# Moving single waits: the order of work in a four-layer graph kernel on one Trainium2 core

## The chip, the cores and the metric

The kernel runs on one core of a Trainium2 chip. A core has a matrix engine (TensorE, PE in the profile; PEld is its weight load), a vector engine (VectorE, DVE), an engine for activations (ScalarE, ACT), a general engine (GpSimd, POOL) and queues that issue DMA transfers; here SyncE (SP) and ScalarE issue them. Each engine runs its own list of instructions in order and waits at semaphores for the others. The metric is the device time of one execution in microseconds (us), the median of several.

## The reference

3327 nodes with 256 features pass four pre-norm residual layers. A is the 3327 x 3327 adjacency matrix `adj`, about 1% of it nonzero.

```python
h = relu(layernorm(x)); x = x + adj @ (h @ W0.T + b0)                              # layer 0
h = relu(layernorm(x)); x = x + relu(top700(tanh(adj*adj)) @ (tanh(h @ Wp + bp) @ Wg) + bg)   # layer 1
h = relu(layernorm(x)); x = x + relu(D**-.5 (adj + I) D**-.5 @ (h @ W2.T))          # layer 2
h = relu(layernorm(x)); x = x + gnn(h)                                              # layer 3

# gnn: two steps
R = (adj + I) / rowsum
for n in range(2):
    logits = (Xa @ W1.T @ W2.T) @ (Xa @ W3.T).T
    A  = softmax(logits) kept to the largest entries that hold 0.9 of the row, renormalised
    Xf = R @ Xf;  Xa = A @ Xa
    Z += Xf @ U1[n].T + Xa @ U2[n].T
gnn = layernorm(h + Z) * g + b
```

D is the row sum of adj + I. All arithmetic that the kernel does on these is float32.

## The kernel before

**Tiles.** The nodes are padded to 26 blocks of 128. Blocks p and p + 13 form *pair* p, so there are 13 pairs. In layers 0 to 2 a pair's rows of `adj` meet the node features as a 2 x 2 block product done with seven block products instead of eight (Strassen in Winograd's form). For that, sums of the four blocks of `adj` are made on VectorE (`Feed.adding`, L552 to L555: s1, a21, s2, s4) and sums of the node blocks once per layer (`combining_nodes`, L367 to L370). The 13 blocks along the inner dimension are cut in three (`CUTS`: 0-5, 5-9, 9-13). So a product of one pair has 91 *units* (7 times 13 matmuls of 128 x 128 x 128), counted 0 to 90; `Product.steps` issues them (L601) in the order 1, 2, 5, 4, 7, 3, 6, in which 5 needs s1, 3 needs s4 and 6 needs s2.

**Loading.** `Feed.upto(n)` keeps the loads two cuts and the sums one cut ahead of the product: it issues the loads of `adj` (L528, four per cut, on SP's queue), then for each load a count of the positive entries where the layer counts (`counter`, L715 to L722, VectorE), then the sums, and stores those sums that layer 3 uses again (L577). `done` (L727, L728) adds a pair's counts with one matmul and copies them out.

**Results.** `Product.result` copies one accumulator bank by ScalarE (L617) and makes the four blocks on VectorE (L622 to L627). Then `finish` adds bias and residual, and the next layer's `Pair` measures and norms its rows (L387, L388, root on POOL L114 and L116, L404; in layer 3 also L459). Its *stages* - turning by TensorE (L416, evicted by L420), projection, and in layer 3 the keys and queries (`keys`, L269, L277, L281) - are hung into the units of the next pair's product by number: `WHERE`, `WHERE_FIRST` for the first pair of a layer, `WHERE_KEYS` in layer 2. In layers 1 and 2 the first cut of pair 1's product is done early, within pair 0's (`early`), since the last node block arrives last.

**Start.** `first_two` runs the first two pairs' products together, in a written order, after `busy` matmuls of the identity (L797) and the 13 pairs' norm, turn and projection.

**Layer 3.** The keys are centred by their mean (`key_sum` L1011 and L1015, `centre` L1022 and L1025). Per row block m of the first step: logits in four chunks (L1045), exponentials by ScalarE (L1070), a search for the threshold (`search_steps`: two passes over the row on ScalarE, L1103 and L1108, or the second on VectorE for row 0, then VectorE L1119 to L1148), then `Rows.begin` transposes the first two groups (L202, copied by ScalarE, L205) and `Rows.finish` does seven groups of matmuls (L213), transposing ahead. In between, `propagate_first` does R @ Xf by pairs in two phases (L1277); `half` (L1286) copies the first bank, and `whole` (L1296 to L1303) makes the blocks. `propagate_first(n, at)` takes a plan: a number k of 26 says behind which share of the phase's units a step is issued. Rows listed in `APART` have no phase behind them and follow each other directly. The second step does the same in the order of pairs, with `finish_pair` or `finish3` making the final layer norm and storing the output (L1397).

**Who sets the order.** TensorE's order is the program's (`tc.manual_schedule(engines=PE_ALONE)`), and so are VectorE's, ScalarE's and SP's inside `first_two`. Elsewhere a planner orders the other engines' instructions before the run, by program order and its own estimate of times; `tc.high_priority()` lifts instructions, and `tc.issue_after(x)` puts those of a block behind x on x's engine.

Of the kernel before, what the change touches and what calls it, by code (L numbers as in the profile page):

```python
# [11 lines left out]
F32 = mybir.dt.float32  # L12
# [5 lines left out]
ALU = mybir.AluOpType  # L18
# [29 lines left out]
def kernel(  # L48
# [243 lines left out]
    def layers_0_to_2(again):  # L292
# [115 lines left out]

        evicted = []

# [23 lines left out]
        class Pair:  # L434
# [17 lines left out]
            def apply(self):  # L452
                if self.layer == 3:
                    self.xn = pair_of(self.rhs.rows, self.p)
                else:
                    self.xn = work.tile([P, 2, D], F32, tag="xn", name=f"xn_{self.name}")
                normed(self.name, self.x2, self.xn, self.mv, self.r, split=self.layer == 0)
                if self.layer == 3:
                    self.made = nc.vector.tensor_scalar(self.xn, self.xn, 0.0, None, ALU.max)  # L459
# [49 lines left out]
        class Feed:  # L509
# [33 lines left out]
            def adding(self, p, c):  # L543
# [12 lines left out]
                if (p, c) in self.keep:  # L556
                    at = self.order.index((p, c))
                    self.made += [(at, s_dram[:, p, n, a:b, :], s) for n, s in enumerate((s1, s2, a21, s4))]
                self.ready[p, c] = a11, a12, s4, a22, s1, s2, a21
                yield last  # L560

# [21 lines left out]
        class Product:  # L583
# [24 lines left out]

            def result(self):

# [5 lines left out]
                with tc.high_priority():  # L616
# [4 lines left out]
                    p1, p2, p5 = (p3[:, n, :P] for n in range(3))  # L621
                    nc.vector.tensor_tensor(u[:, 2, :], p1, b[:, 0, :], ALU.add)  # L622
                    nc.vector.tensor_tensor(u[:, 1, :], u[:, 2, :], b[:, 1, :], ALU.add)
# [8 lines left out]
        WHERE = {2: (60, 84), 3: (48, 61, 76), 6: (12, 22, 34, 46, 58, 70)}  # L632
        WHERE_KEYS = (74, 89)
        WHERE_FIRST = {2: (58, 86), 3: (52, 70, 89)}

        def products(layer, width, rhs, feed, finish, before, pair_after, following=None, counted=None, begin=None):
# [5 lines left out]
            for p in range(H):  # L642
# [4 lines left out]
                else:  # L647
# [36 lines left out]
                    feed.upto(n)  # L684
                y, p3 = prod.result()
                x2 = feed.x2.pop(p)
# [18 lines left out]
        def counter(i):  # L705
# [18 lines left out]
            def done(p):  # L724
                m = p + i * H
                pc = bank(f"pc_{m}")
                nc.tensor.matmul(pc[:, :1], sums.pop(p)[:, 0, :], ones, start=True, stop=True)  # L727
                nc.vector.tensor_copy(counts[:, m : m + 1], pc[:, :1])  # L728

# [30 lines left out]
        if not again:  # L760
# [33 lines left out]
            def first_two(product):  # L794
                busy = bank("busy")
                for _ in range(12):
                    nc.tensor.matmul(busy[:, :P], ident, ident, start=True, stop=True)  # L797
                with tc.manual_schedule(engines=IN_FIRST_TWO):
                    return first_two_in(product)

            def first_two_in(product):
                for a, b in ((0, 1), (1, 2), (2, 4), (4, 6), (6, 9), (9, 12), (12, 13)):
# [38 lines left out]
                for p in range(H):  # L841
                    pairs[p].turn()
                    if p + 3 < H:
                        pairs[p + 3].measure()
# [31 lines left out]
                count()  # L876
                feed.to_count = None
                feed.upto(5)
                work_of(4)
                work_of(5)  # L880
                return len(order), prods

# [97 lines left out]
    def layer_3_in(again, tag, big, ep, w3, sm3, h3, kT0, ksum0, left):  # L980
# [244 lines left out]
        class PropagatedPair:  # L1225
# [79 lines left out]

            def ended(self):
                with tc.high_priority():
                    nc.vector.tensor_tensor(self.y[:, 1, :], self.y[:, 1, :], self.accs[2][:, :P], ALU.add)

# [90 lines left out]

        ys, stores = {}, []

        def finish_pair(p, both, pair):
# [162 lines left out]
        with tc.manual_schedule(engines=PE_ALONE):  # L1566
# [88 lines left out]
            for i in range(EARLY):  # L1655
# [11 lines left out]
                elif i == 1:  # L1667
                    steps = prepare(0, 0, kT0)
                    centred = {4: [lambda: centre(kT0, mean0(), "0"), lambda: next(sums_of_first)]}
                    propagate_first(1, merged(centred, whole_run(steps, 10), plan))  # L1670
                    run(find(0, 0, st0))
# [11 lines left out]
            for m in range(T):  # L1683
# [7 lines left out]
                if m + AHEAD < T and not interleaved:  # L1691
                    plan = merged(plan, {4: [lambda: next(prepare(0, m + AHEAD, kT0))]})
                a = AttentionOfFirstStep(m, rows.finish(m, plan), dens.pop(m), f"{m}")
                if interleaved:
# [57 lines left out]
        with tc.manual_schedule(engines=PE_ALONE):  # L1752
# [31 lines left out]
            for i, m in enumerate(ORDER):  # L1784
                ahead = ORDER[i + AHEAD] if i + AHEAD < T else None
                plan, later = passes_apart(1, finder) if ahead else (passes(finder), {})
                if i == 0:
                    p, q = props
                    plan = merged(plan, {5: [p.scale, q.scale]})
                    of_next = {2: [p.turn], 5: [q.turn], 10: [p.sums], 14: [q.sums]}  # L1790
# [29 lines left out]
                else:  # L1820
# [104 lines left out]
```

## Time and profile before

| | |
|---|---|
| time, median of 3 | 2533.23 us (2530.99 to 2536.49) |
| profiled execution: its time / its span | 2532.95 us / 2531.1 us |
| TensorE busy | 2493.5 us |
| VectorE busy | 2093.9 us |
| ScalarE busy | 1085.2 us |
| POOL busy | 297.7 us |
| layers 0 to 2 | until about 949 us |
| first step of layer 3 | until about 1804 us |
| second step, and the end | until 2531 us |
| last matmul ends | 2519.75 us |
| mean granted TensorE clock | 0.996 |

In a profile line a time stands first as the start in us from the span's beginning, then the duration, engine, line of the kernel, operation, tiles written and read, shapes. `[1.04 <-ACT eT_a L205]` behind it is how long the engine sat idle just before and what released it. A matmul of float32 is recorded as two passes, so one unit is "x2". PEclk is the TensorE clock granted, 1.00 is full.

### The profile page before, as it was taken

How to read it: one execution, taken by the hardware profiler on the slowest of the kernel's cores; microseconds unless marked ns; L12 is line 12 of the kernel's file. 1: busy time of each engine (PE TensorE's matmuls, PEld its weight loads, DVE VectorE, ACT ScalarE, POOL GpSimd, SP SyncE). 2: the span in 40 equal slices, each digit the busy share in tenths (PEclk: the TensorE clock that was granted, in tenths of full speed). 3: DMA queues.
4: the chain of work that ended last, by engine and by line, in shares of the span. 5: the costliest groups of instructions: out<-in, count | busy, mean ns of one | idle time of the engine just before them, and what ended most of it. 6: DMA issues, size and time to landing. Idle time of an engine off the chain costs nothing.

```text
span 2531.1 us, 47787 instructions
## 1 busy us (share of the span) xinstructions
PE 2493.5 (99%) x17953; PEld 2257.0 (89%) x17953; DVE 2093.9 (83%) x5534; ACT 1085.2 (43%) x2158; POOL 297.7 (12%) x463
## 2 busy tenths in 40 slices
PE   9999999999999999999999999999999999999998
PEld 8999999999999998888887888888888888888887
DVE  7777788888877878788879797884999999999995
ACT  3011023444111105565656565663655555565551
POOL 2000010000000001000000000000022222222222
PEclk9999999999999999999999999999999999999999
DMA  6677665555698867323132323133434343344333
GB/s 195 212 225 244 220 207 171 180 173 178 228 314 276 272 224 228 98 82 107 57 112 87 109 84 104 55 107 107 164 104 129 108 132 125 108 127 139 123 114 107
DMA packets 181774, 388.28 MB, mean 153 GB/s; under 512 B 19741, under 2 KB 78746, under 8 KB 181530
## 3 DMA queue, kind: packets, MB, share of 16 engines
q1 hardware_dynamic: 153210, 364.31, 44.5%
q10 hardware_dynamic: 28320, 20.80, 2.6%
q8 instruction: 143, 2.34, 0.4%
q14 instruction: 101, 0.83, 0.1%
HBM read 315.44 MB, written 67.89 MB: 151 GB/s over the span
## 4 chain that ended last, share of the span: by engine, by line
PE 59%; ACT 2%; DVE 1%; issue 0%; POOL 0%; POOLq 0%; DVEq 0%; ACTq 0%
PE a L213 23%; PE f1a L1277 10%; PE f0a L1277 9%; PE pl_a L1045 6%; PE pt_a L202 6%; PE u L1361 2%; PE u L1331 2%; PE f L1204 1%; ACT junk_a L1108 1%; PE pkq L269 0%; ACT junk_a L1103 0%; PE pt_a L162 0%; PE pt_f L162 0%; ACT eT_a L205 0%; ACT e_a L1070 0%
## 5 line engine op out<-in xcount | busy, mean ns | idle before, releaser
L205 ACT COPY eT_a<-pt_a 128x512 f32<-128x512 f32 (+1 forms) x364 | 196.6, 555 | 374.5 <-PE pt_a L202 373.3
L213 PE MATMUL a<-h3a,eT_a 128*128 128x256 f32 x1352 | 324.1, 381 | 1.7 <-ACT eT_a L205 1.7
L213 PE MATMUL a<-vs,eT_a 128*128 128x256 f32 x1352 | 320.3, 381 | 1.3 <-ACT eT_a L205 1.3
L1132 DVE MAX8 cand_a<-w 128x8 f32<-128x128 f32 x1352 | 287.9, 278 | 4.3
L213 PEld LDWEIGHTS a<-h3a,eT_a 128*128 128x128 f32 x1352 | 243.9, 189 | 35.7 <-ACT eT_a L205 3.4
L601 PE MATMUL acc_a<-tsa,s_a 128*128 128x128 f32 (+1 forms) x2028 | 272.5, 276 | 2.7 <-DVE s_a L552 2.7
L213 PEld LDWEIGHTS a<-vs,eT_a 128*128 128x128 f32 x1352 | 244.8, 190 | 31.6 <-ACT eT_a L205 2.0
L601 PEld LDWEIGHTS acc_a<-tsa,s_a 128*128 128x128 f32 x2028 | 250.8, 193 | 3.5 <-DVE s_a L552 2.9
L601 PE MATMUL acc_a<-tsa,a_a 128*128 128x128 f32 x2028 | 249.6, 275 | 0.0
L601 PE MATMUL acc_a<-rhs,a_a 128*128 128x128 f32 (+1 forms) x2028 | 248.5, 276 | 0.7 <-ACT rhs L490 0.7
L601 PEld LDWEIGHTS acc_a<-tsa,a_a 128*128 128x128 f32 x2028 | 239.0, 192 | 0.6
L601 PEld LDWEIGHTS acc_a<-rhs,a_a 128*128 128x128 f32 x2028 | 236.4, 192 | 1.6 <-ACT rhs L490 1.1
L1128 DVE SCALAR_TENSOR_TENSOR w<-e_a,t_a 128x896 f32<-128x896 f32 x208 | 225.5, 1084 | 3.0
L1246 POOL TENSOR_TENSOR slab3a<-slab3a,ident 128x128 f32<-128x128 f32 x100 | 109.8, 1098 | 911.2 <-DMA slab3a<-in_adj_t_dram 340.3
L1070 ACT ACTIVATE e_a<-pl_a 128x1024 f32<-128x1024 f32 x260 | 184.7, 728 | 43.8 <-PE pl_a L1045 38.3
L202 PE MATMUL pt_a<-ident,e_a 128*128 128x128 f32 x1352 | 198.6, 272 | 0.2
L1119 DVE SCALAR_TENSOR_TENSOR w<-e_a,t_a 128x3328 uint8<-128x3328 f32 x52 | 191.6, 3685 | 4.7 <-DVE t_a L1116 0.5
L1148 DVE SCALAR_TENSOR_TENSOR e_a<-e_a,all_least 128x3328 f32<-128x3328 f32 x52 | 192.1, 3694 | 1.8
L202 PEld LDWEIGHTS pt_a<-ident,e_a 128*128 128x128 f32 x1352 | 165.4, 141 | 29.4 <-ACT eT_a L205 2.6
L745 ACT ACTIVATE a_a<-a_a 128x640 f32<-128x640 f32 (+1 forms) x156 | 101.4, 666 | 170.1 <-DVE a_a L743 149.4
L420 ACT ACTIVATE xT_a<-pt_a 128x512 f32<-128x512 f32 x52 | 30.8, 593 | 334.0 <-PE pt_a L416 271.6
L1277 PE MATMUL f0a<-tsa,slab3a 128*128 128x128 f32 x1352 | 165.9, 276 | 0.0
(256 smaller groups left out, 4226.0 us busy)
## 6 DMA issues: line engine op xcount, KB each, us to landing
slab3a<-s_dram SPq DMA_DIRECT2D x100, 832.0 KB, 4.5
a_a<-in_adj_t_dram SPq DMA_DIRECT2D x312, 256.0 KB, 4.3
slab3a<-in_adj_t_dram SPq DMA_DIRECT2D x79, 832.0 KB, 4.6
a_a<-in_adj_t_dram SPq DMA_DIRECT2D x156, 320.0 KB, 3.9
s_dram<-s_a SPq DMA_DIRECT2D x78, 256.0 KB, 4.8
s_dram<-s_a SPq DMA_DIRECT2D x39, 320.0 KB, 4.7
x_dram<-x_a ACTq DMA_DIRECT2D x39, 256.0 KB, 3.2
s_dram<-a_a SPq DMA_DIRECT2D x26, 256.0 KB, 5.2
```

The lines of the kernel that those rows point to most:

```text
L202: nc.tensor.transpose(pt[:, j, :], e[:, k * P : (k + 1) * P], ident)
L205: last_turned.append(nc.scalar.copy(eT[:, : len(blocks), :], pt[:, : len(blocks), :]))
L213: nc.tensor.matmul(acc[:, :width], ready[g][:, j, :], rhs[:, k, :], start=(k == 0), stop=(k == T - 1))
L601: nc.tensor.matmul(self.acc[:, g, at : at + wide], quads[n][:, k - CUTS[c][0], :], t, start=(k == 0 and n in (1, 4)), stop=(k == H - 1 and ...
L1045: nc.tensor.matmul(parts[h], q[h * DA : (h + 1) * DA, :], kT[h * DA : (h + 1) * DA, a:b], start=True, stop=True,)
L1070: last_exp.append(nc.scalar.activation(dst, src, AF.Exp, accum_out=parts[:, c : c + 1]))
L1119: nc.vector.scalar_tensor_tensor(junk, e, t, e, ALU.is_lt, ALU.mult, accum_out=got)
L1128: nc.vector.scalar_tensor_tensor(w[:, : (b - a) * P], eg, t, eg, ALU.is_lt, ALU.mult, accum_out=below[:, g : g + 1])
L1132: nc.vector.max(cand[:, 8 * k : 8 * k + 8], w[:, (k - a) * P : (k - a + 1) * P])
L1148: nc.vector.scalar_tensor_tensor(e, e, least, e, ALU.is_ge, ALU.mult, accum_out=st["kept"][:, m : m + 1])
L1246: added.append(nc.gpsimd.tensor_tensor(x[:, p, :], x[:, p, :], ident, ALU.add))
L1277: nc.tensor.matmul(self.accs[bank][:, c * P : (c + 1) * P], a, self.right(n, k), start=start, stop=last.get(bank) == (n, k), skip_group_ch ...
```

## The change

1. Twelve identity matmuls at the start become 15, and four more are issued behind the first pair's turn.
2. In the first two pairs' written order, the third pair's sums are put ahead of the counts of its loads, which now come behind both products' last cuts; the first result's first sum (L622) is issued behind those sums.
3. The copy of a count (L728) gets high priority.
4. The last pair's `hidden` and `second` stages in layer 1's first product move from units 70 and 89 to 66 and 83.
5. In layers 1 and 2, at the end of the first pair, the feed goes one cut further before the result, and that pair's norm (L404) is issued behind the sums so added.
6. In layer 2 the turn and the keys move from units 74 and 89 to 81 and 90.
7. In layer 3's second phase, the keys' mean moves from 4 to 7.5 of 26 and row 0's logits from 10 to 14.5.
8. For rows of the first step that follow each other, `rows.begin(m + 1)` moves into the row before, behind its sixth group of matmuls.
9. Between the steps, the second row's logits move from 0 to 8 of 26, and the scale, turn and sums there from 3, 8, 12 to 9, 16, 20.
10. In the second step's first row, the first pass of the search for the third row moves from behind group 0 to behind group 4.
11. At the end, the last pair's two rows: the first is stored at once, and the last row is done by `finish_last`, which takes the row's second half with the last bank added straight into z, so that `ended` (L1308) falls away, and makes the statistics by halves.

```diff
-        evicted = []
+        evicted, hold = [], []
...
-                normed(self.name, self.x2, self.xn, self.mv, self.r, split=self.layer == 0)
+                with tc.issue_after(hold[-1].ins) if hold else nullcontext():
+                    normed(self.name, self.x2, self.xn, self.mv, self.r, split=self.layer == 0)
...
+                self.added = last
                 yield last
...
-            def result(self):
+            def result(self, behind=None):
...
-                    nc.vector.tensor_tensor(u[:, 2, :], p1, b[:, 0, :], ALU.add)
+                    with tc.issue_after(behind.ins) if behind else nullcontext():
+                        nc.vector.tensor_tensor(u[:, 2, :], p1, b[:, 0, :], ALU.add)
...
-        WHERE_KEYS = (74, 89)
-        WHERE_FIRST = {2: (58, 86), 3: (52, 70, 89)}
+        WHERE_KEYS = (81, 90)
+        WHERE_FIRST = {2: (58, 86), 3: (52, 66, 83)}
...
-                y, p3 = prod.result()
+                hold[:] = []
+                if early and p == 0:
+                    feed.upto(n + 1)
+                    hold.append(feed.added)
+                y, p3 = prod.result(feed.added if begin and p == 0 else None)
...
-                nc.vector.tensor_copy(counts[:, m : m + 1], pc[:, :1])
+                with tc.high_priority():
+                    nc.vector.tensor_copy(counts[:, m : m + 1], pc[:, :1])
...
-                for _ in range(12):
-                    nc.tensor.matmul(busy[:, :P], ident, ident, start=True, stop=True)
+                def warm_up(n):
+                    for _ in range(n):
+                        nc.tensor.matmul(busy[:, :P], ident, ident, start=True, stop=True)
+                warm_up(15)
...
                     pairs[p].turn()
+                    if not p:
+                        warm_up(4)
...
                 count()
-                feed.to_count = None
                 feed.upto(5)
                 work_of(4)
                 work_of(5)
+                while feed.to_count:
+                    count()
+                feed.to_count = None
...
-            def ended(self):
-                with tc.high_priority():
-                    nc.vector.tensor_tensor(self.y[:, 1, :], self.y[:, 1, :], self.accs[2][:, :P], ALU.add)
...
+        def finish_last(m, y, rows, acc, name, behind):
+            z = w3.tile([P, D], F32, tag="z", name=f"z1_{name}")
+            x3 = w3.tile([P, NC, P], F32, tag="hT", name=f"x3_{name}").rearrange("p c n -> p (c n)")
+            with tc.issue_after(behind.ins):
+                nc.sync.dma_start(z, z_dram[:, m, :])
+                nc.sync.dma_start(x3, x3_dram[:, m, :])
+            nc.gpsimd.tensor_tensor(z, z, y, ALU.add)
+            nc.gpsimd.tensor_tensor(x3, x3, bs, ALU.add)
...
+            with tc.high_priority():
+                nc.vector.scalar_tensor_tensor(z, rows, by, z, ALU.mult, ALU.add)
+                nc.vector.bn_stats(st[:, 0, :], z[:, :P])
+                nc.vector.scalar_tensor_tensor(z[:, P:], acc, by, z[:, P:], ALU.mult, ALU.add)
+                nc.vector.bn_stats(st[:, 1, :], z[:, P:])
+                nc.vector.bn_aggr(mv3, st)
+                nc.vector.tensor_scalar(r, mv3[:, 1:2], EPS, None, ALU.add)
+            rsqrt(r, r)
+            nc.vector.scalar_tensor_tensor(z, z, mv3[:, 0:1], gs, ALU.subtract, ALU.mult)
+            nc.vector.scalar_tensor_tensor(z, z, r, x3, ALU.mult, ALU.add)
+            nc.sync.dma_start(out[m * P : (m + 1) * P, :], z)
...
-                    centred = {4: [lambda: centre(kT0, mean0(), "0"), lambda: next(sums_of_first)]}
-                    propagate_first(1, merged(centred, whole_run(steps, 10), plan))
+                    centred = {7.5: [lambda: centre(kT0, mean0(), "0"), lambda: next(sums_of_first)]}
+                    propagate_first(1, merged(centred, whole_run(steps, 14.5), plan))
...
+                alone = not interleaved and m != T - 3 and m + 1 < T
+                if alone:
+                    plan = merged(plan, {5: [lambda: rows.begin(m + 1)]})
...
-                elif m + 1 < T:
-                    rows.begin(m + 1)
+                elif alone:
                     left_over = {0: [a.turn], 1: [a.node], 3: [a.values]}
...
-            propagate_first(T - 2, merged(whole_run(steps_of_second, 0), {3: [lambda: p.scale(last_exp)], 8: [p.turn], 12: [p.sums]}))
+            propagate_first(T - 2, merged(whole_run(steps_of_second, 8), {9: [lambda: p.scale(last_exp)], 16: [p.turn], 20: [p.sums]}))
...
-                    plan = merged(plan, {5: [p.scale, q.scale]})
+                    plan = merged({4: plan[0]}, {5: [p.scale, q.scale]})
...
-                            stores.append(finish3(m, ys.pop(m), both[:, 1, :], f"{m}", pair.loaded))
-                            pair.ended()
-                            stores.append(finish3(p, ys.pop(p), both[:, 0, :], f"{p}", pair.loaded))
+                            finish3(m, ys.pop(m), both[:, 1, :], f"{m}", pair.loaded)()
+                            finish_last(p, ys.pop(p), both[:, 0, :], pair.accs[2][:, :P], f"{p}", pair.loaded)
```

More of the change, by code (lines that the diff above doesn't have):

```diff
@@ L795, in first_two, with first_two_in @@
                 busy = bank("busy")
-                for _ in range(12):
-                    nc.tensor.matmul(busy[:, :P], ident, ident, start=True, stop=True)
+                def warm_up(n):
+                    for _ in range(n):
+                        nc.tensor.matmul(busy[:, :P], ident, ident, start=True, stop=True)
+                warm_up(15)
                 with tc.manual_schedule(engines=IN_FIRST_TWO):
-                    return first_two_in(product)
-            def first_two_in(product):
+                    return first_two_in(product, warm_up)
+            def first_two_in(product, warm_up):
                 for a, b in ((0, 1), (1, 2), (2, 4), (4, 6), (6, 9), (9, 12), (12, 13)):
@@ L1401, in layer_3_in @@
         ys, stores = {}, []
+        def finish_last(m, y, rows, acc, name, behind):
[6 more added lines that the diff above has]
+            nc.gpsimd.tensor_tensor(x3, x3, bs, ALU.add)
+            st = sm3.tile([P, 2, 6], F32, tag="st3", name=f"st3_{name}")
+            mv3 = sm3.tile([P, 2], F32, tag="mv3", name=f"mv3_{name}")
+            r = sm3.tile([P, 1], F32, tag="r3", name=f"r3_{name}")
+            by = rinv[:, m : m + 1]
+            with tc.high_priority():
[9 more added lines that the diff above has]
+            nc.sync.dma_start(out[m * P : (m + 1) * P, :], z)
         def finish_pair(p, both, pair):
```

## The prediction

> **What bounds the kernel.** I read the page's busy table first, then TensorE's waits, then its timeline around each wait, then the granted clock by window. The page:
>
> ```profile
> span 2531.1 us, 47787 instructions
> PE 2493.5 (99%) x17953; PEld 2257.0 (89%) x17953; DVE 2093.9 (83%) x5534; ACT 1085.2 (43%) x2158; POOL 297.7 (12%) x463
> ```
>
> TensorE is idle for 2531.1 - 2493.5 = 37.6 us in all. Its last matmul ends at 2519.75, so 11.4 us of that are the tail; the rest are single waits, which the view of waits lists (engine, line, who released it; total us, times, longest us):
>
> ```profile
> PE pt_a L416 <- DVE xn_a L404: 3.5, 3, 1.9
> PE pt_a L416 <- DVE h3a L459: 3.1, 2, 1.6
> PE pl_a L1045 <- ACT e_a L1070: 3.0, 1, 3.0
> PE a L213 <- ACT eT_a L205: 3.0, 9, 1.0
> PE acc_a L601 <- DVE s_a L555: 3.0, 3, 2.4
> PE acc_a L601 <- DVE s_a L552: 2.7, 1, 2.7
> PE pk_mean_0a L1011 <- DVE ktotal_0a L1015: 1.5, 1, 1.5
> ```
>
> No wait repeats row by row, except 0.24 to 0.29 us in eight attention rows. So the change can be costed wait by wait. Each wait may cost twice, since the clock can fall behind it. The windows view (stretch; length, PE busy, instructions, granted clock, DMA share, GB/s), cut at the clock's own steps:
>
> ```profile
> 8.10:11.52 3.42, 1.67 (x8) 1.00 1.06 358
> 11.52:14.93 3.41, 3.41 (x11) 0.50 1.11 326
> 697.60:701.01 3.41, 1.05 (x10) 1.00 1.01 358
> 701.01:704.42 3.41, 3.41 (x17) 0.50 0.96 329
> 786.34:789.75 3.41, 1.78 (x17) 1.00 0.06 22
> 789.75:793.16 3.41, 3.41 (x31) 1.00 0.88 245
> ```
>
> A stretch busy for 1.67 us or less is followed by 3.41 us at half clock, which loses 1.7 us; one busy for 1.78 is not. The same follows the waits at 83.83 and 1772.06. Four such stretches cost 6.8 us.
>
> **A rule against this.** The Trainium skill, page "TensorE: Matmul & The Clock Gate", section "Why this matters for your kernels", asks only for no idle gaps above about 3 us, and its Part 1 lets the clock fall after a whole idle window of 3.4 us. By that, none of our gaps but 3.01 us comes near, the warm-up matmuls buy nothing, and the sum below would be 13.5 instead of 18.6 us (2519.5 us). The rows show the fall at half an idle window; I take the rows. That page also says the window runs free of the kernel, so the cost differs by run: a gap of g us between 1.7 and 3.4 fills half a window in g/3.41 of the alignments, my estimate from the 3.41 us above.
>
> **The change, part by part** (gain in us; a unit is one 128-wide matmul, 0.223 us from "x10 1.28" rows).
>
> 1. *Warm-ups.* 3 + 4 identity matmuls are 14 passes of 0.11 = 1.6 us, inside the idle 5.97-7.12 and 7.86-9.81, which stay: both end with xn (L404), which waits for x landing at 6.0 and 8.7. If x came sooner, they would cost up to 1.6. The second gap shrinks to about 1.0 us, so the half clock at 11.52 goes: -1.7 (0 to -1.9). It carries on: VectorE has 0.6 to 1.0 us free per pair until 21.7, then needs 2.18 per pair against TensorE's 2.17.
>
> 2. *Third pair's sums.* The wait at 83.83 (2.66 us) is for L552, which ran at 85.63 behind two counts; the first count reuses the buffer that the count matmul at 81.30 frees. The inputs had landed by 71.0. Put ahead, the sums run from 72.5; L554 waits for the product that ends at 75.05, so L555 ends at 76.5-77. The first result (u, L622, 75.77 before) is queued behind it: 1.3 us later, and behind u the finish, the statistics, the normed pair and its x1 store. Its accumulator is needed at 81.36 only; its turn comes at unit 12, about 84.2, and xn (81.77 before) is ready by 83.1-84.2 with u of the second pair and the counts in between. I keep 0.3 of a wait: -(2.66 + 1.7 - 0.3) = -4.0 (-2.3 to -4.4).
>
> 3. *Layer 1's start.* The count's copy now goes first, but the 0.70 us at 352.77 has a second releaser: the weights come from h2T, whose tanh ends at 353.23 for a load at 353.43. -0.1. The 0.73 us at 382.72 waits for the last pair's projection; issued 6 units (1.3 us) sooner, its copy (L490, 382.81) ends before it is wanted, if tanh L483 (379.25) moves with it: -0.6 (0 to -0.73).
>
> 4. *Sums ahead of the normed pair in layers 1 and 2.* In layer 1, s4 then fills VectorE's 0.91 us wait for the root: -0.5. In layer 2, s4 (L555, 700.15) is wanted at 698.52; wait 2.36 plus 1.7 of clock. Four loads and two counts of the next cut come ahead too. The sums' inputs landed by 690.2 and their buffers are free once stores land at 691.0-693.4, so s4 is there by 695. But these 2.6 us of VectorE go ahead of the finish: the count matmul's wait at 693.45 grows from 0.32 to about 1.0, and h3a (698.1 before) is late by some 1 us at its turn, which must no longer wait at 698.52 but comes at 699.4. -(4.06 - 1.7) = -2.4 (-0.4 to -4.1).
>
> 5. *Keys' turn at 81 for 74.* 7 units are 1.56 us; the two waits are 1.63 and 1.43: -2.9. The keys' matmuls at 90 leave 9 units, 2.0 us, for a copy that ends 1.3 us after the turn starts; the two hT stores and two qT stores on ScalarE's queue move along, in a layer where ScalarE is mostly idle.
>
> 6. *Keys' sum at 7.5, logits at 14.5.* The 1.46 us at 961.79 vanish, since 7 units take 1.56. But the logits still wait for the centred keys (L1025 ends at 967.38), so the exponentials and row 0's first pass stay where they are:
>
> ```profile
> 974.29 3.07 ACT L1103 ACTIVATE junk_a<-e_a,t_a 128x3328 uint8<-128x3328 f32 x1
> 977.27 0.19 ACT L1103 ACTIVATION_READ_ACCUMULATOR junk_a<-e_a,t_a 128x1 f32 x1
> 977.65 0.59 ACT L1286 COPY xf_0a<-f0a 128x512 f32<-128x512 f32 x1 [0.20 <-PE f0a L1277]
> ```
>
> The phase now has 22 units behind the logits for 31: it ends at 970.42 + 4.9 + 0.3 = 975.6 for 977.61. The copy L1286 that frees its bank is then caught behind the pass until 977.46, so TensorE waits from 975.6 to 978.1 (0.68 us before, now 2.5): net -0.2, and that wait brings the half clock, +1.7. I take +1.5 (-1.5 to +1.7). Were the copy put first, the pass and row 0 would be 1.9 us late, and row 0 has 1.86 us between its last search (L1148, 1007.12) and its first transpose (1008.99): also about nothing gained.
>
> 7. *Attentions that follow each other.* Six waits (five of 0.24, one of 0.29): the next row's 8 transposes and two copies now precede the last 4 matmul passes (0.86 us), which cover the copy (0.59). Their e is ready 3.7 us ahead at the least. -1.4.
>
> 8. *Logits between the steps.* At 1772.06 the fourth logits wait 3.01 us: ScalarE runs row 0's pass (L1103, 1770.85-1774.0) before it empties the bank. At unit 16 they start at 1773.0, the exponentials at 1774.2 as before. Scale, turn (2 transposes, a copy) and sums (4 matmuls, copy, one store) follow at 1779.6 and 1781.6 with inputs at 1778.7 and 1780.2. The phase takes 52 x 0.223 + 3.0 + 1.9 = 16.5 for 21.5 us. Late next: row 0's e (1799.7, does not move) for transposes then wanted at 1799.4. -(5.0 - 0.4) = -4.6 (-2.5 to -5.0). Slabs are released sooner too; each lands 4.5-5.2 us after issue and still before its use.
>
> 9. *Row 0 of the second step.* The pass L1103 (1813.90) kept copy L205 for 1.04 us; behind the last copy it delays the two scales instead, wanted 0.1-0.5 later: -0.7.
>
> 10. *End by halves.*
>
> ```profile
> 2520.05 0.28 DVE L1308 TENSOR_TENSOR xf_1a<-xf_1a,f1a 128x128 f32<-128x128 f32 x1
> 2523.78 0.48 DVE L1389 SCALAR_TENSOR_TENSOR z<-z,r,x 128x256 f32<-128x256 f32 x1 [0.78 <-POOL r L116]
> ```
>
> From the last matmul to z are 4.2 us. By halves: add 0.29, statistics of 128 columns (0.18 to 0.43, no row; 0.25), aggregate 0.18, eps 0.15, power 0.58, z 0.48, with handovers 2.1. The other row's four operations (1.57) and its power on POOL compete for the same time, which leaves between -0.9 and -2.1: -1.2. The stores are the same three.
>
> **Sum:** 1.7 + 4.0 + 0.7 + 0.5 + 2.4 + 2.9 - 1.5 + 1.4 + 4.6 + 0.7 + 1.2 = 18.6. The profiled execution took 2532.95 (span 2531.1 and 1.85 around it), 0.3 below the median 2533.23: 2514.3 us.
>
> **Rivals.** *All of it comes through* (0.12): nothing new waits and part 6 pays: 27.3 us, 2505.6. For it: the covers above are long; against: part 6's copy is 0.2 us from the pass today. *Waits come back* (0.15): the first turns of parts 2 and 4 and the bank of part 6 each wait above 1.7 us and draw the half clock again; 8 to 11 us remain, 2522 to 2525. For it: VectorE is full from 690 to 702. *It doesn't do what it says* (0.07): the orders on VectorE and ScalarE outside the written parts come from a planner whose clock is not the chip's; the gains are offset, 2528 to 2538. *Slower* (0.05): a shifted plan puts a pass L1103 ahead of a copy L205 in every row of the second step, as at 1813.90 in one: 25 x 1.04 = 26 us, 2540; it decides from 18.6 / 25 = 0.75 us a row. Against it: these rows run without one TensorE wait today, with row after row alike.
>
> **How the numbers follow.** The likeliest (0.61) is 2514.3, alone 2510 to 2519. Four in five lie in 2507 to 2523: the likeliest, most of the first rival and the near part of the second. Runs of this kernel tell 0.2% (5 us) from no change, so faster 0.89, same 0.06, slower 0.05.
>
> **What would show it.** Granted clock 1.00 from the first turns to 900; no L601 wait for L552; L416 waits for h3a gone at p above 1; at 975 a wait f0a <- xf_0a of 2 to 2.5 us (this one proves part 6 right); one short L202 wait for L1148 near the second step; copies L205 releasing two waits for nine; DVE's last z some 2.5 to 3.3 us after the last matmul. Wrong: any wait that repeats per row, or a half clock in layers 0 to 2.

## The result, and the profile after

| | before | after |
|---|---|---|
| time, median (us) | 2531.98 (6 runs, 2529.15 to 2536.49) | 2517.91 (6 runs, 2516.8 to 2521.5) |
| profiled execution: time / span (us) | 2532.95 / 2531.1 | 2517.92 / 2516.1 |
| TensorE busy (us) | 2493.5 | 2486.4 |
| last matmul ends (us) | 2519.75 | 2504.86 |
| from there to the end of the span (us) | 11.40 | 11.26 |

The ratio is 0.9945 (95%: 0.9933 to 0.9958): 14.1 us less. The forecast was 2514.3 us, 18.6 us less. The page of the changed kernel (span, then busy time by engine):

```profile
span 2516.1 us, 47844 instructions
PE 2486.4 (99%) x17967; PEld 2254.9 (90%) x17967; DVE 2095.5 (83%) x5536; ACT 1086.3 (43%) x2158; POOL 296.9 (12%) x462
```

Its view of TensorE's waits (engine, line, releaser; us in all, times, longest):

```profile
PE pt_a L416 <- DVE xn_a L404: 5.4, 4, 2.1
PE pt_a L416 <- DVE h3a L460: 2.9, 1, 2.9
PE f0a L1293 <- ACT xf_0a L1302: 2.4, 1, 2.4
...
PE pc L734 <- DVE pos L729: 1.5, 1, 1.5
...
PE hid_a L478 <- ACT xT_a L420: 0.8, 1, 0.8
PE a L213 <- ACT eT_a L205: 0.5, 2, 0.2
PE pt_f L162 <- ACT xf_0a L1364: 0.4, 1, 0.4
PE pt_a L202 <- DVE e_a L1164: 0.3, 1, 0.3
```

No wait for a sum s_a is left, nor the one for the logits' bank. But several lines are new or larger. The line of xn (L404) now includes the first pair's turn in the third product of layer 0 at 83.22 (1.45 us) and layer 1's first turn at 398.69 (2.09); h3a is layer 2's first turn at 696.91 (2.92). The count matmul (L734) waits 1.49 us where it waited 0.32, and the copy xf_0a comes 2.41 us late for 0.68. The windows view, cut at the clock's steps (stretch; length, PE busy, PE's loads, DVE, ACT, POOL, granted clock, DMA share, GB/s), says what these cost besides:

```profile
397.36:400.77 3.41, 1.33 (x12) 1.14 (x11) 2.50 (x9) 1.89 (x3) 1.28 (x2) 1.00 0.93 286
400.77:404.19 3.42, 3.42 (x16) 3.38 (x17) 2.99 (x6) 1.67 (x4) 0.00 (x0) 0.50 0.35 101
697.73:701.14 3.41, 1.30 (x12) 1.31 (x13) 2.87 (x6) 0.55 (x1) 0.20 (x1) 1.00 1.00 372
701.14:704.56 3.42, 3.42 (x19) 3.42 (x18) 3.39 (x10) 0.53 (x2) 0.00 (x0) 0.50 0.93 260
967.38:970.80 3.42, 1.73 (x16) 1.53 (x14) 3.18 (x2) 3.29 (x3) 0.31 (x3) 1.00 0.83 271
970.80:974.21 3.41, 2.70 (x18) 2.13 (x20) 3.22 (x9) 0.66 (x3) 0.52 (x1) 1.00 0.55 211
```

Both first turns draw a half clock, 1.7 us each. The wait for xf_0a of part 6 (2.41 us, forecast 2 to 2.5) does not: its stretch is busy for 1.73 us.

The same matmul's start in both traces gives each part's share (us, after less before). The parts are numbered as in the prediction. Its part 4 is the fifth in the list of changes, and is the one meant where an expectation below speaks of the fifth part or of part 5.

| part | forecast | measured |
|---|---|---|
| 1 warm-ups | -1.7 | -1.3 (x came 0.4 later) |
| 2 third pair's sums | -4.0 | -2.8 |
| 3 layer 1's start | -0.7 | -0.6 (count -0.5, hooks -0.1) |
| 4 in layer 1 | -0.5 | +3.2, and -1.65 later in the layer |
| 4 in layer 2 | -2.4 | +1.7 |
| 5 keys' turn | -2.9 | -3.5 |
| 6 keys' sum, row 0's logits | +1.5 | -1.1 |
| 7 attentions that follow | -1.4 | -3.0 |
| 8 logits between the steps | -4.6 | -4.45 |
| 9 row 0 of the second step | -0.7 | -0.7 |
| 10 end by halves | -1.2 | -0.1 |
| elsewhere in layers 2 and 3 | | -0.7 |
| sum | -18.6 | -15.0 |

The sum is that of the two profiled executions; the medians differ by 14.1.

### The profile page after: what moved, and what is told of

Its sections match the earlier page's. It is cut to its first block, busy times and chain, and to the rows that moved or that the text cites. A ratio compares the mean times of both kernels' runs of the same rounds, so it can differ in the third digit from the quotient of the medians.

```text
span 2516.1 us, 47844 instructions
## 1 busy us (share of the span) xinstructions
PE 2486.4 (99%) x17967; PEld 2254.9 (90%) x17967; DVE 2095.5 (83%) x5536; ACT 1086.3 (43%) x2158; POOL 296.9 (12%) x462
## 5 line engine op out<-in xcount | busy, mean ns | idle before, releaser
L205 ACT COPY eT_a<-pt_a 128x512 f32<-128x512 f32 (+1 forms) x364 | 196.7, 555 | 375.9 <-PE pt_a L202 372.6
L1262 POOL TENSOR_TENSOR slab3a<-slab3a,ident 128x128 f32<-128x128 f32 x100 | 115.0, 1150 | 900.1 <-DMA slab3a<-in_adj_t_dram 383.7
L420 ACT ACTIVATE xT_a<-pt_a 128x512 f32<-128x512 f32 x52 | 30.9, 595 | 355.7 <-PE pt_a L416 321.4
```

What stands on the lines that cost most here:

```text
L205: last_turned.append(nc.scalar.copy(eT[:, : len(blocks), :], pt[:, : len(blocks), :]))
L1262: added.append(nc.gpsimd.tensor_tensor(x[:, p, :], x[:, p, :], ident, ALU.add))
```

## Experiments

Each ratio is against the kernel before in the same set of runs. In every experiment but the last its interval overlaps the changed kernel's (0.9933 to 0.9958), and some kernels have a single run; there a difference of medians is a pointer only, and the reading rests on the trace.

### Clock: warm-ups undone, and waits filled

```diff
-                warm_up(15)
+                warm_up(12)
...
-                    if not p:
-                        warm_up(4)
```

> The changed kernel with the warm-up matmuls of the kernel before (12, and none behind the first turn). By the half-window rule of the rows, the second of the two waits for xn grows by about 0.9 us and a stretch with 1.75 us or more of idle comes back: 3.41 us at half clock in the first 16 us, and the first product begins 1.3 to 1.7 us later after the second turn than with 15 and 4. By the page's rule (3 us, or a whole idle window) the granted clock stays at 1.00 there and nothing moves.

The profiled execution took 2519.84 us. Its windows view:

```profile
7.08:10.49 3.41, 1.10 (x8) 0.66 (x7) 2.19 (x9) 0.95 (x3) 1.42 (x3) 1.00 1.01 289
10.49:13.91 3.42, 3.40 (x10) 2.59 (x9) 3.22 (x15) 1.84 (x4) 2.21 (x5) 0.50 1.07 356
```

The half clock is back behind a single gap of 2.31 us, and the first product begins 1.57 us later after the second turn than in the changed kernel. The rule read from the rows holds. That of the Trainium skill's page "TensorE: Matmul & The Clock Gate" (no gaps above about 3 us, section "Why this matters for your kernels") does not: this gap is shorter.

```diff
+                        def turn_filled(turn=todo[0]):
+                            fill = bank(f"fill_{layer}")
+                            for _ in range(8):
+                                nc.tensor.matmul(fill[:, :P], ident, ident, start=True, stop=True)
+                            turn()
-                        hooks, carried = {86: todo[0]}, {14: todo[1]}
+                        hooks, carried = {86: turn_filled}, {14: todo[1]}
```

> The changed kernel, with eight identity matmuls (16 passes of 0.11 us, 1.76 us) issued ahead of the first pair's turn in layers 1 and 2, in the time in which it waits. Half-window rule of the rows (a stretch of 3.41 us with 1.7 or more of idle brings one at half clock): idle falls to 0.3 and 1.2 us, the clock stays at 1.00, each turn keeps its time and what follows gains 1.7 us: -3.4 us, of which layer 1 may give back up to 1.6; 2514.5 to 2516. The page's rule (only a gap above 3 us or a whole idle window): gaps of 2.09 and 2.92 us were not the cause, the half clock comes again or had never followed from them: 2517.9.

Median 2515.88 us (4 runs, ratio 0.9932, 0.9917 to 0.9947), 2.0 less than the changed kernel. In its trace the listed waits at the two turns are down to 0.24 and 1.25 us, the clock is 1.00 through layers 0 to 2, and layer 1 gives back 0.9 us before its end. The clock behind the two waits followed the idle time of its stretch, as the rows have it. What the waits themselves are worth is the next question.

### Part 4: without the sums ahead

```diff
-                if early and p == 0:
-                    feed.upto(n + 1)
-                    hold.append(feed.added)
```

> The changed kernel without its fifth part (no sums ahead of the first pair's result in layers 1 and 2, no hold). Theory A, the sums put ahead take VectorE's time from the first pair's finish, so its turn waits and draws the half clock: the waits of 2.09 and 2.92 us for xn and h3a and both stretches at half clock go; the kernel before's 0.5 us (layer 1) and 2.4 us with a half clock (layer 2) for s4 come back. Product 3 of layer 1 begins 3.2 us sooner than in the changed kernel; up to 1.6 of it is waited for again by the end of layer 1, whose last turn has 0.26 us to spare; layer 2 gives 1.6 more. In all -1.5 to -3.1 us, 2514.8 to 2516.4. Theory B, the prediction's part 4 was right and something else made the two turns late: +2.9 us, 2520.8.

Median 2513.99 us (4 runs, ratio 0.9928, 0.9914 to 0.9943), 3.9 less: theory A, by more than it asked for. Timed again beside the changed kernel:

> The changed kernel as it is, as a yardstick on the same chip for the three beside it. Both theories of part 5: 2516.5 to 2518.5 us; layer 1's first turn waits 1.5 to 2.1 us, layer 2's 2.9 to 4.3.

> Once more the changed kernel without its fifth part, now timed beside the changed kernel. If the part costs what one profile of each said (A): 3 to 5 us less than the changed kernel, about 2514; the waits for s4 of 1.2 us in layer 1 and 2.4 in layer 2 are back, the first turns do not wait. If that was only the luck of which wait drew a half clock (B): within 1.5 us of it.

2517.85 us for the changed kernel (5 runs, ratio 0.9948, 0.9935 to 0.9962) and 2515.26 without the part (5 runs, 0.9943, 0.9930 to 0.9957). The medians differ by 2.6 us here, between the two theories, and by 3.9 in the first comparison. The intervals overlap, so that the part loses rests on the traces together with these. Waits of the first kernel without it:

```profile
PE acc_a L603 <- DVE s_a L556: 3.9, 3, 2.5
PE f0a L1290 <- ACT xf_0a L1299: 2.4, 1, 2.4
PE pt_a L416 <- DVE xn_a L404: 1.8, 2, 1.5
```

The sums are waited for again (1.25 us in layer 1, 2.45 in layer 2), and no first turn of these layers waits. Against the changed kernel, layer 1 gains 2.4 us from its first to its fourth product and keeps 2.2 of it to its end; layer 2 gains 3.2. The hold itself is without effect: with it alone taken out, every engine's list of instructions is the same, so this was not run. What costs is the further cut.

Why, the changed kernel's timeline in layer 2 shows (start, us, engine, line; L722 and L724 count, L553 to L556 are the sums, L404 and L460 the norm):

```profile
693.52 0.49 DVE L722 TENSOR_SCALAR pos<-a_a 128x640 bf16<-128x640 f32 x1 [0.33 <-DMA a_a<-in_adj_t_dram]
693.93 0.42 DVE L387 BATCH_NORM_STATS2 st_a<-x_a 128x6 f32<-128x256 f32 x1
694.27 0.81 DVE L724 SCALAR_TENSOR_TENSOR pos<-a_a,pos 128x640 bf16<-128x640 f32 x1
...
695.40 0.81 DVE L553 TENSOR_TENSOR s_a<-a_a,a_a 128x640 f32<-128x640 f32 x1
...
696.24 0.82 DVE L554 TENSOR_TENSOR a_a<-a_a,a_a 128x640 f32<-128x640 f32 x1
697.97 0.74 DVE L404 TENSOR_SCALAR h3a<-x_a,mv_a,r_a 128x256 f32<-128x256 f32 x2 [0.91 <-POOL r_a L116]
698.62 0.82 DVE L555 TENSOR_TENSOR s_a<-s_a,a_a 128x640 f32<-128x640 f32 x1
699.36 0.42 DVE L460 TENSOR_SCALAR h3a<-h3a 128x512 f32<-128x512 f32 x1
```

The sums that TensorE wants at 695.86 end at 691.08. But by then the feed stands a cut further on: between the finish and the norm VectorE does the counts and sums of the third pair (640 columns: its first cut), waits 0.33 us for a load, and still stands empty for 0.91 us behind the root. That load (issued 689.25, landed 693.50) decides how late the turn is. In the seven profiles that have this order and no other edit at the turn, VectorE waited 0.27 to 1.87 us for it at the count, and TensorE's wait at the turn was 2.59 or 2.60 us longer than that in each: 2.92 us for 0.33 here, 4.46 for 1.87 when the changed kernel was timed again (above the 4.3 expected).

### Part 4: the turn later

```diff
-                        hooks, carried = {86: todo[0]}, {14: todo[1]}
+                        hooks, carried = {}, {5: todo[0], 20: todo[1]}
```

> The changed kernel, with the first pair's turn in layers 1 and 2 moved from unit 86 of the second pair's product to unit 5 of the third's (10 units, 2.2 us later), its projection from 14 to 20. Theory A, only the turn is too early and VectorE's order stays: layer 1's wait of 2.09 us and layer 2's 2.92 shrink to 0 and 0.7 us, neither draws the half clock: -3.8 and -3.9 us. Of layer 1's share up to 1.6 is given back at later turns. In all -6.0 to -7.7, near 2511. Theory B, VectorE bounds these layers: what the turn wins is waited for at the next sums or turns, in all less than 2 us, 2516 or more.

Median 2515.59 us (6 runs, ratio 0.9930, 0.9918 to 0.9942), 2.3 less. Neither theory has it whole. Both turns' shares came (layer 1's third product 4.0 us ahead, layer 2's another 3.9), but layer 1 gave 3.3 of its 4.0 back and layer 2 about 2.3. Before layer 1's later turns, xn was ready 2.77, 2.47, 2.46 us ahead in the changed kernel, running down to 0.26 at the last; here 0.14, 0.24, 0.42, and mostly 0.06. So with the feed's order of part 4, VectorE sets the pace of the layer, and what TensorE does not wait for at the first turn it waits for at the next. The kernel without the part kept its gain through the same layer. Why VectorE stays behind for 12 pairs after an order that differs only at the start was not settled.

### Part 4: sums in the root's shadow

Only layer 2: the next cut's sums are issued between the first pair's statistics and its norm, with no loads and no counts.

```diff
-                if early and p == 0:
-                    feed.upto(n + 1)
-                    hold.append(feed.added)
+                def add_next():
+                    feed.add(*feed.order[feed.done[1]])
+                    feed.done[1] += 1
+                    hold.append(feed.added)
+                waiting[:] = [add_next] if early and p == 0 and layer == 2 else []
...
                     self.measure()
+                    while waiting:
+                        waiting.pop()()
                     self.apply()
```

> The changed kernel without its fifth part; in layer 2 alone, the sums of the next cut (no loads, no counts) are put between the first pair's statistics and its norm. Theory A, part 5 failed because it pulled the sums and another cut's counts ahead of the whole finish, while 0.9 us of VectorE stand empty behind the statistics: the sums end by 691 in the time of the kernel without the part (wanted at 692), h3a is 0.5 to 1.3 us later, within its slack of 1.3: the wait of 2.45 us goes and at most 0.5 us of a new one comes: 2 to 2.5 us less than without the part, 2 to 4 less if the half clock went with it, 2510 to 2512. Theory B, VectorE is full there and any order of the same work costs the same: a wait for h3a of 2 us or more, no gain over the kernel without the part.

Median 2512.58 us (5 runs, ratio 0.9930, 0.9917 to 0.9944), 2.7 less than without the part: theory A. The intervals overlap, but each of the five runs took less than each of the five without the part. Its timeline (line numbers are shifted there: L555 to L558 are the sums, L727 counts):

```profile
686.40 0.66 DVE L555 TENSOR_TENSOR s_a<-a_a,a_a 128x512 f32<-128x512 f32 x1
686.98 0.18 DVE L388 BATCH_NORM_AGGREGATE mv_a<-st_a 128x2 f32<-128x6 f32 x1
687.10 0.69 DVE L556 TENSOR_TENSOR a_a<-a_a,a_a 128x512 f32<-128x512 f32 x1
687.71 0.68 DVE L557 TENSOR_TENSOR s_a<-s_a,a_a 128x512 f32<-128x512 f32 x1
688.38 0.49 DVE L727 TENSOR_SCALAR pos<-a_a 128x640 bf16<-128x640 f32 x1
688.78 0.69 DVE L558 TENSOR_TENSOR s_a<-a_a,s_a 128x512 f32<-128x512 f32 x1
689.39 0.73 DVE L404 TENSOR_SCALAR h3a<-x_a,mv_a,r_a 128x256 f32<-128x256 f32 x2
```

No idle time stands before L404: the sums fill what the root takes (0.91 us), s4 ends at 689.47 for a matmul at 690.29, and h3a at 691.19 for a turn at 691.25. Both waits are gone, the half clock with them. What part 4 was meant for was there to be had; its order was not.

### Part 2: counts behind the norm

```diff
-                while feed.to_count:
-                    count()
-                feed.to_count = None
...
                 first = pair
+                if begin and p == 0:
+                    with tc.issue_after(pair.applied.ins):
+                        while feed.to_count:
+                            feed.to_count.pop(0)()
+                    feed.to_count = None
```

> The changed kernel, with the counts of the third pair's loads, which part 2 left ahead of the first pair's norm on VectorE, issued behind that norm (L404). Theory A, the wait of 1.45 us for xn at the first turn of layer 0's third product is VectorE's order alone (root done at 82.73, L404 issued at 84.22 behind two counts and the second pair's blocks): the wait falls to 0.2 to 0.8 us and the fourth product begins 0.7 to 1.2 us sooner after the third. Theory B, the statistics, the root or the result are late themselves: the wait stays within 0.2 us of 1.45.

One run, read from its trace: the wait falls from 1.45 to 0.11 us, and the fourth product begins 1.43 us sooner. That is theory A, above its upper end. The changed kernel's timeline has what stood ahead:

```profile
82.48 0.68 DVE L724 SCALAR_TENSOR_TENSOR pos<-a_a,pos 128x512 bf16<-128x512 f32 x1
...
83.61 0.68 DVE L724 SCALAR_TENSOR_TENSOR pos<-a_a,pos 128x512 bf16<-128x512 f32 x1
84.22 0.73 DVE L404 TENSOR_SCALAR xn_a<-x_a,mv_a,r_a 128x256 f32<-128x256 f32 x2
```

The root was done at 82.73, the turn wanted xn at 83.22.

### Part 6: the copy ahead of the pass

```diff
-                    run(find(0, 0, st0))
+                    finder = find(0, 0, st0)
+                    next(finder)
+                    with tc.issue_after(halves_copied[-1].ins):
+                        next(finder)
+                    run(finder)
```

> The changed kernel, with row 0's first pass over its scores (L1119, ScalarE) issued behind the copy of the bank (L1302) that TensorE waits 2.41 us for. Theory A, row 0's search is the chain that ends last there (its e is ready 0.45 us before its first transpose): the pass starts 1.9 us later, TensorE's wait of 2.41 goes, and a wait for row 0's e of 3.4 to 3.8 us takes its place, with a half clock behind it: +1.4 to +3.1 us, 2519.3 to 2521. Theory B, the wait of 2.41 is on the path: -2.4 us, 2515.5.

Median 2520.27 us (4 runs, ratio 0.9951, 0.9936 to 0.9966), 2.4 more, as theory A has it. The waits of its profiled execution, at 2515.21 us the fastest of the four by 4.7:

```profile
...
PE pt_a L202 <- DVE e_a L1164: 2.8, 2, 2.3
...
PE f0a L1295 <- ACT xf_0a L1304: 0.7, 1, 0.7
```

The wait for the copy falls from 2.41 to 0.68 us and TensorE comes 1.7 us sooner to the next phase; then row 0's e is 2.33 us late, with a half clock behind it, and 3.9 us are lost by row 1. So 2.1 us are lost there in all, in an execution that is faster elsewhere: its waits in layers 1 and 2 drew no half clock. In the changed kernel e stands ready only 0.45 us ahead of row 0: all but that 0.45 of the 2.41 us that TensorE waits for the copy would be waited for at row 0 instead.

### Part 8 undone

```diff
-            propagate_first(T - 2, merged(whole_run(steps_of_second, 8), {9: [lambda: p.scale(last_exp)], 16: [p.turn], 20: [p.sums]}))
+            propagate_first(T - 2, merged(whole_run(steps_of_second, 0), {3: [lambda: p.scale(last_exp)], 8: [p.turn], 12: [p.sums]}))
```

> The changed kernel with part 8 undone (the second row's logits between the steps at 0 of 26 again, scale, turn and sums at 3, 8 and 12). Theory A, the part gave what the trace says: the fourth logits wait 3.0 us for ScalarE behind row 0's pass, a half clock follows where the stretch has 1.75 us or more of idle, and row 26 begins 4.4 us later than in the changed kernel (2.7 without the half clock). Theory B, row 0's e bounds there and the phase was hidden behind it: row 26 begins at most 1 us later.

One run, 2520.85 us: row 26 begins 4.34 us later than in the changed kernel, counted from row 0. Theory A. Its waits hold the line of the kernel before again, with a half clock behind it (a stretch with 2.87 us idle):

```profile
PE pl_a L1061 <- ACT e_a L1086: 3.0, 1, 3.0
```

### Part 10: the last store on ScalarE

```diff
-            nc.sync.dma_start(out[m * P : (m + 1) * P, :], z)
+            nc.scalar.dma_start(out[m * P : (m + 1) * P, :], z)
```

> The changed kernel with the store of the last row issued by ScalarE instead of SyncE. Theory A, that store lands late (2.7 us after its issue, 2.0 before the change) because it is queued on SyncE behind the two stores of the other row: it lands 2.0 us after issue, the span ends 0.7 us sooner after the last matmul. Theory B, the stores share the DMA engines, whatever queue they come from, and the last lands about 1.1 us after the one before it: still 2.7 us, no gain.

From the last matmul to the end of the span are 8.54 us for 11.26: 2.7 less, where A expected 0.7 and B none: neither had the cause. The store lands 2.06 us after issue, but that is not the gain: it took 1.85 to 3.0 in the kernels that leave it on SyncE, and their spans end 10.8 to 11.4 us after the last matmul whatever it took. The store's issue in both timelines, changed kernel and this one:

```profile
2507.97 0.48 DVE L1438 SCALAR_TENSOR_TENSOR z<-z,r,x 128x256 f32<-128x256 f32 x1 [0.45 <-POOL r L116]
2508.49 0.54 SPq L1439 DMA_DIRECT2D out_dram<-z  x1
```

```profile
2511.06 0.36 ACTq L1439 DMA_DIRECT2D out_dram<-z  x1
```

At the end each engine reads a flag (0.5 us) and branches on it; the trace has SyncE's branch at 2509.70 and its next instruction at 2512.24, then a list of final waits that stands still once more for 1.9 us, until 2514.55. That list sets the end. With the store elsewhere, SyncE branches before the store is issued; its list then ran without the second stop, and the span ended 4.92 us after the store's issue for 7.63. The second stop, 1.2 to 1.9 us, is in each of the 12 profiles with the store on SyncE and in neither of the two without. In the changed kernel the semaphore at that place was complete at 2511.22, when the store had landed, so it is not the landing. But the packed traces hold transfers of 8 KB that are marked as instructions. In each of the 12, one of them ends 1.1 to 1.3 us before SyncE goes on; in all 14, one ends 1.1 to 1.3 us before SyncE's first instruction behind the branch. So the engine may be waiting for its code at both stops. No run varied this, and it is not shown.

### All together

Sums in the root's shadow, counts behind the norm, the last store on ScalarE.

> The one before with the third pair's counts behind the first pair's norm and with the last row's store on ScalarE. If the three gains are independent of each other (A), 1.2 to 1.4 us for the counts and 2.4 to 2.8 for the store come on top: 3.6 to 4.2 us less than the one before, near 2507. If VectorE's backlog takes the counts' share back in layers 0 to 2 (B): 2.4 to 2.8 us less.

Median 2507.34 us (4 runs, ratio 0.9910, 0.9895 to 0.9925): 5.2 us less than sums in the root's shadow alone (A, and more), 10.5 less than the changed kernel in the same set, whose interval (0.9935 to 0.9962) lies clear of it. Page and waits:

```profile
span 2502.4 us, 47840 instructions
...
PE f0a L1301 <- ACT xf_0a L1310: 2.4, 1, 2.4
PE busy L818 <- POOL ident masks.py:199: 1.5, 1, 1.5
PE pl_a L1069 <- ACT qT L281: 1.3, 4, 0.3
PE hid_a L481 <- ACT xT_a L421: 0.8, 1, 0.8
PE acc_a L606 <- DVE s_a L559: 0.5, 1, 0.5
```

In the profiled execution (2504.25 us, the fastest of the four) the clock is 1.00 up to the tail. Part of that is luck: the wait of 2.41 us for xf_0a is still there and drew no half clock.

## Why the prediction was right, and where it was not

The time fell within the range, 3.6 us above the forecast. The path it argued on, TensorE's single waits and the clock behind them, was the right one. That the sum came so near is luck in part: part 4 missed by 6.1 us and parts 2 and 10 by 1.2 and 1.1, while parts 6, 7 and 5 gave 2.6, 1.6 and 0.6 us more than forecast. Of its signs, the waits for L552 and for h3a above pair 1 are gone, and the copies L205 release two waits for nine, as said. The sign of being wrong that it named, a half clock in layers 0 to 2, came twice, both times behind part 4.

Two of its sums do not come out. Under the Trainium skill's rule (no gaps above about 3 us, on the page and in the section named at warm-ups undone) part 6 would have no half clock either, so the total there is 15.2 us and not 13.5. That is nearer to the measured 14.1 than 18.6 is; it is the rows above, not the total, that decide between the rules. And the upper ends of its parts add up to 25.3 us, where the first rival has 27.3.

1. *Warm-ups* (-1.7, got -1.3): right. Undone, they cost 1.57 us; x came 0.4 us later in the changed kernel's profile.
2. *Third pair's sums* (-4.0, got -2.8): the wait and its half clock went as said. The step that failed is xn "is ready by 83.1-84.2 ... I keep 0.3 of a wait": between the root and L404 ran two counts and the second pair's blocks, and xn was complete at 84.95. The wait was 1.45 us.
3. *Layer 1's start*: the total held, its halves did not. The copy of the count was worth 0.5 us and not 0.1; the earlier hooks 0.1 and not 0.6, since `hidden` now waits 0.80 us for ScalarE's copy of xT (L420).
4. *Sums ahead* (-2.9 for both layers, got +4.9, of which 1.65 was recovered): wrong in sign. "h3a (698.1 before) is late by some 1 us at its turn" was the failing step. It counted 2.6 us of VectorE ahead of the finish, and took the wait for the next cut's load at nothing. But a count of the third pair stood ahead of the first pair's statistics until its load had landed, and two sums of that pair followed before the norm: h3a was complete at 699.78 for a turn wanted at 696.91, 2.92 us, and the half clock stayed. For layer 1 the sum saw only the empty 0.91 us behind the root, and no late turn at all; it came to 2.09 us, and a half clock. The 1.65 us recovered there are waits of the kernel before at five later turns of layer 1, which a TensorE 3 us further back no longer meets. Its list has only two of them, with 0.40 and 0.15 us; from start to start they cost 0.1 to 0.7 us each.
5. *Keys' turn* (-2.9, got -3.5) and 7. *attentions that follow* (-1.4, got -3.0): the mechanism was right, the size was read from the list of waits, which is short by some 0.2 us a time. The two kernels' timelines (before, then after) at one of the six rows:

```profile
1126.61 1.03 PE L202 MATMUL pt_a<-ident,e_a 128*128 128x128 f32 x8
1127.89 1.99 PE L213 MATMUL a<-h3a,eT_a 128*128 128x256 f32 x8 [0.24 <-ACT eT_a L205]
```

```profile
1118.98 1.04 PE L202 MATMUL pt_a<-ident,e_a 128*128 128x128 f32 x8
1119.85 2.76 PE L213 MATMUL a<-h3a,eT_a 128*128 128x256 f32 x12
```

From the transposes to the matmul are 1.28 us before and 0.87 after: 0.41 for a listed 0.24, since the list begins at the modelled end of the last transpose. The first pass behind the wait then takes 0.32 us for 0.22. That makes 0.5 a row.

6. *Keys' sum* (+1.5, got -1.1): the wait came as forecast, 2.41 us, the clock did not. A stretch of the clock cut it so that 1.69 us of idle fell into one. In 7 of 12 profiles with this wait the half clock did come, which fits the prediction's estimate (g/3.41, 0.7). So the forecast took the likelier case, and its absence here is luck. The rest of the miss is in the logits:

```profile
966.41 4.09 PE L1045 MATMUL pl_a<-kT_0a,qT 64*128 64x512 f32 x16
```

```profile
960.93 3.07 PE L1061 MATMUL pl_a<-kT_0a,qT 64*128 64x512 f32 x16
```

In the kernel before, the second half of the centred keys (L1025) is there at 967.38 only. Until then the two halves of a logit, which otherwise start together, run one by one: 1.0 us within a group of matmuls, which no list of waits shows. That nothing would be gained "were the copy put first" was right: it loses.

8. *Logits between the steps* (-4.6, got -4.45) and 9. *row 0 of the second step* (-0.7): right, with what comes late next as named: 0.34 us for row 0's e (0.4 forecast) and 0.40 for the scale (0.1 to 0.5).
10. *End by halves* (-1.2, got -0.1): from the last matmul to the last store's issue, 4.54 us became 3.62, so the halves gave 0.9. (The 4.2 us that the prediction counts to z are 4.51 to the end of z in its own row.) "The stores are the same three" was the step that failed: what follows the store took 7.63 us for 6.86. The sum had ended at z, while SyncE's work behind the store sets the end.

Of the rivals, "waits come back" took place in part: the waits that it named came (1.45, 2.09, 2.92 and 2.41 us), the two of part 4 drew the half clock, and what parts 5 to 8 gave above the forecast made up for most of it. No wait that repeats by row appeared.

## What to carry to other kernels

Before work is pulled ahead of a finish, list what else the call that pulls it issues, which of that waits for a load, and whether an order that is written down binds anything. Here a hold changed no instruction, and the counts and loads that came with the sums cost more than the sums gave. Fill the empty time behind a long handover with just the operations that the next wait needs. Read a wait's price from start to start of the same matmuls, and cut the windows at the clock's own steps before a half clock is charged to it.

## What was not expected of the hardware

- **The clock.** In the 14 profiles, up to the last matmuls, some 40 stretches of 3.41 us with 0.9 to 1.73 us of TensorE idle had none at half clock behind them, 21 with 2.04 to 3.39 us all had one, and of six between 1.75 and 1.96 three had. The length of a gap alone does not decide: one of 3.47 us (copy put first, layer 2), cut into 1.80 and 1.66 by the stretches, drew none, and one of 1.78 us (last store on ScalarE, layer 1) drew one. And the stretches lie differently in each execution: the same first turn in layer 1 waited 1.5 to 2.1 us in six profiles of the same code and drew the half clock in three of them.
- **The end.** After the flag's branch the next instruction came 2.5 to 3.2 us later, on SyncE, VectorE and GpSimd alike and in every kernel. A store ahead of that branch on SyncE cost 2.7 us more than one on ScalarE (11.26 us from the last matmul to the end of the span for 8.54).
